# A graph network in fp32: the order of seven products in Strassen's scheme, where their running sums are kept, and 64-column weights for two small products

## The chip, the core and the metric

The kernel runs on one core of a Trainium2 chip. The core has five engines with a queue of instructions each: TensorE (PE) multiplies matrices into PSUM, loading its weights (PEld) beside the multiplications; VectorE (DVE), ScalarE (ACT) and GpSimd (POOL) work element by element; SyncE (SP) issues the transfers (DMA). Engines wait for each other through semaphores, and each engine takes its instructions in the order in which they were written. SBUF is the working memory, PSUM has eight banks of 128 x 512 fp32 words.

The metric is the time of one execution on the device in microseconds, as the median of several runs. A profile is taken of one execution; its span runs from the first instruction to the last.

## What is computed

A chain of four graph layers on x of 128 graphs x 64 nodes x 512 features, with an adjacency matrix adj of 64 x 64 for each graph. Every layer normalizes first, h = max(layernorm(x), 0), and adds its result to x. Cut to what matters:

```python
# layer 0: H = (adj != 0); M = Dn H Be H^T
y = M @ (layernorm(relu(M @ (h @ W1.T) + b1)) @ W2.T) + b2
x = x + y + h
# layer 1: attention weights A (64 x 64) of tanh, leaky relu, exp, adj
x = x + A @ h @ w
# layer 2: attention with adj
q, k, v = h @ Wq.T + bq, h @ Wk.T + bk, h @ Wv.T + bv
p = adj * exp(q @ k.T)
x = x + (p / p.sum(-1)) @ v
# layer 3: transition T (64 x 64); Xk = T^k h
x = x + relu(sum_k(Xk @ Wk[k] + bk[k]))        # k = 0, 1, 2
```

All of it is in fp32.

## The kernel before

Four tiles of 128 tokens (two graphs each) make a group, and there are 16 groups. Layers 0 and 1 go over all groups first and leave x in DRAM (`xmid`); then layers 2 and 3 go over all groups. Large products of two token tiles by a weight matrix are done by Winograd's form of Strassen's scheme: each factor is cut in 2 x 2 blocks, and seven products of blocks stand for eight. A group needs eight such schemes: two each for W1 (512 columns a product), W2 and W (256 columns), then one for q (with the weights Wq and Wk multiplied beforehand, WG) and one for v, both with four multiplications of 256 columns a product. Layer 3 uses the scheme twice over, 7 x 7 products of 128 x 128 blocks for the three weight matrices at once (`product`, L1089), with the factors kept in DRAM (`fac`) and loaded for each use (L1081).

A scheme's left factors are made by four additions on VectorE (`strassen`, `comb`, L642): s1, s2, one in place, and s4. `seven` (L608 to L630) then orders the seven products and the way to the four results. It takes four PSUM banks, p1 to p4. A first product is copied to SBUF by ScalarE (L618) as U0. The sixth goes to p2, and VectorE adds U0 to it as U1 (L620); the seventh goes to p4, and VectorE adds U1 to it as U2 (L622). The second adds to p1 in PSUM, and the result (0,0) is emitted from p1. The fifth goes to p3, and with U2 gives result (1,1). The fourth adds to p4, the third to p3, and these with U1 give (1,0) and (0,1). Three products thus add to a bank that holds an earlier one, and each waits until that one has been read. What an emission does is the caller's: `scaled` with `emit_z` for W1 (L668, L670, relu at L776), `biased` for W2 (GpSimd at L678, VectorE at L680), `emit_w` for W (L842, L843), `emit_q` (L902, L908, L911) and `emit_v` (L951, L953). For q the first copy carries a bias (`first`, L919), and the bias of the other half is mended in two additions with `gb_d`.

The matrix M of layer 0 is made by four multiplications a group (L748, 128 x 128 weights, 65 columns, one for each tile), and T^2 of layer 3 likewise (L1014). Both weights are block diagonal: two graphs of 64 nodes a tile. `left_mul_T` (L586) multiplies h by such a matrix, L801 multiplies y by M, L930 makes the logits of layer 2 with 64-column weights for each half, L1035 multiplies by T and T^2 with 64 rows, L968 multiplies by v. `transposed` turns a tile by a ScalarE copy (L595), a transposing transfer and another copy (L597).

The order of all instructions is settled before the program is written. Each operation is put into a graph with an engine, an assumed cost and a priority; the priority is a running time (`step`) plus a shift for each named part (`AT`) and a period for each group. `Graph.run` goes through a list schedule: it takes the operation that can start earliest by the assumed costs, by priority among equals, and hands out the buffers, PSUM banks too. So a change of one cost or one shift moves instructions on every engine, and the engines then keep to that order whatever they meet. Where the plan leaves TensorE idle for over half a microsecond, `fill` puts multiplications by ones (L1156) there.

Of the kernel before, what the change touches and what calls it, by code (L numbers as in the profile page):

```python
# [14 lines left out]
P = 128  # L15
C = 64
# [152 lines left out]
def tile_adj_preln_d4(  # L169
# [81 lines left out]
    def c_mm(n, count):  # L251
        return 2 * count * max(n * 2 / 2400 + 0.0045, 0.1115)

# [20 lines left out]
    def quad(b):  # L274
# [4 lines left out]

    STRETCH, PERIOD1, PERIOD2 = (3.2256, 5.2241, 17.5226, 2.1512), 108.846, 147.837  # L280
    AT = {
        "x0": -2785.77, "apart": 476.78, "w1": 74.24, "b1": -151.66, "w2": 219.46, "w": 134.54, "c1": 30.0, "l0":
        161.71, "c2": -499.09, "l1": 200.03, "c": 636.68, "g0": -1635.76, "g1": -1647.49, "g2": -1525.11, "g3":
        -1533.9, "g": -74.06, "bq": 140.69, "l3": -1075.2, "wg": -359.01, "wp": 397.89, "beg0": -349.29, "beg1":
        -79.14, "end00": -7.47, "end01": -453.12, "end11": 445.06, "new2": -58.97, "new3": 65.85, "end2": -38.2,
        "end3": 52.04, "load1": -441.32, "load2": -33.39, "m": 8.52, "h0": 1.51, "p0": 16.02, "z0": -2103.65, "q0":
        141.1, "y0": 43.5, "h1": -50.95, "p1": -14.39, "z1": 175.87, "q1": 18.24, "y1": -606.44, "s": 17.3, "t0":
        -515.12, "e0": -376.27, "t1": -24.41, "e1": -275.63, "hT": -120.44, "sh": 574.26, "lq": 31.03, "pt": -20.86,
        "v": -19.97, "pv": -240.05, "s3": 152.28, "tt": 14.82, "a0": 226.63, "b0": -282.82, "a1": 284.86, "ws":
        172.31, "load3": 413.3,  # L290
    }
# [85 lines left out]
    gb_c = const.tile([P, KD], F32, name="gb_c")  # L377
    gb_d = const.tile([P, 2], F32, name="gb_d")
    wg_d = dram.tile([D, D], F32, name="wg_d")

    def dot(in0, in1, acc, r, w):
        j = Buf("o")
        dve(0.77, lambda: nc.vector.scalar_tensor_tensor(j.t, in0(), 1.0, in1(), op0=ALU.mult, op1=ALU.mult,
                                                         accum_out=acc()), r, [*w, j])
# [93 lines left out]
    def setup_bq():  # L478

        pg, bk = Buf("ps"), Buf("o")  # L480
        for o in range(KD):
            k_ = temp(Wk[o * P:(o + 1) * P, :])
            if o == 0:
                dve(0.45, lambda k_=k_: nc.vector.tensor_scalar(bk.t, k_.t, bq_c[:, 0:1], None, op0=ALU.mult), [k_, "bq_c"], [bk])
            else:
                dve(0.77, lambda o=o, k_=k_: nc.vector.scalar_tensor_tensor(bk.t, k_.t, bq_c[:, o:o + 1], bk.t, op0=ALU.mult, op1=ALU.add),
                    [k_, "bq_c", bk], [bk])

        def mg():
            for c in range(KD):  # L490
                nc.tensor.matmul(pg.t[:, c:c + 1], bk.t[:, c * P:(c + 1) * P], ones[:, 0:1], start=True, stop=True)
        pe(c_mm(1, KD), mg, [bk], [pg])
        dve(0.2, lambda: nc.vector.tensor_copy(gb_c, pg.t[:, :KD]), [pg], ["gb"])
        dve(0.16, lambda: nc.vector.tensor_sub(gb_d, gb_c[:, 0:2], gb_c[:, 2:4]), ["gb"], ["gbd"])

# [56 lines left out]
    def norm_stats(src, k, r):  # L552

        st, mv, rs = Buf("st"), Buf("mv"), Buf("rs")
        for i in range(k):
            dve(0.69, lambda i=i: nc.vector.bn_stats(st.t[:, i, :], src(i)), [r[i]], [(st, i)])  # L556
        dve(0.19, lambda: nc.vector.bn_aggr(mv.t, st.t[:, :k, :].rearrange("p k s -> p (k s)")), [(st, i) for i in range(k)], [mv])  # L557
        pool(0.32, lambda: nc.gpsimd.tensor_scalar_add(rs.t, mv.t[:, 1:2], EPS), [mv], [rs])  # L558
        pool(0.65, lambda: nc.gpsimd.tensor_tensor(rs.t, rs.t, mhalf, ALU.pow), [rs], [rs])  # L559
        return mv, rs  # L560

    def offset(mv, rs):
        nm = Buf("nm")
        pool(0.47, lambda: nc.gpsimd.tensor_scalar(nm.t, mv.t[:, 0:1], rs.t, -1.0, op0=ALU.mult, op1=ALU.mult), [mv, rs], [nm])  # L564
        return nm
# [41 lines left out]

    def seven(mul, U, n, emit, first=None):  # L608

        p1, p2, p3, p4 = (Buf("ps") for _ in range(4))
        at = lambda i: (lambda: U.t[:, i, :n])
        mul[1](p1, True)
        if first:
            first(p1)
        else:
            act(n / 1200 + 0.17, lambda: nc.scalar.copy(at(0)(), p1.t[:, :n]), [p1], [(U, 0)])  # L618
        mul[6](p2, True)
        dve(c_v(n), lambda: nc.vector.tensor_add(at(1)(), p2.t[:, :n], at(0)()), [p2, (U, 0)], [(U, 1)])  # L620
        mul[7](p4, True)
        dve(c_v(n), lambda: nc.vector.tensor_add(at(2)(), p4.t[:, :n], at(1)()), [p4, (U, 1)], [(U, 2)])  # L622
        mul[2](p1, False)
        emit(0, 0, p1, None, (U, 0))
        mul[5](p3, True)
        emit(1, 1, p3, (U, 2), (U, 2))
        mul[4](p4, False)
        emit(1, 0, p4, (U, 1), (U, 0))
        mul[3](p3, False)
        emit(0, 1, p3, (U, 1), (U, 1))  # L630

    def strassen(A, keys, B, kc, n, stag, emit, outs=None):
# [8 lines left out]
        def comb(d, kd, x_, kx, y_, ky, op):  # L641
            dve(c_v(kc * P), lambda: nc.vector.tensor_tensor(d(), x_(), y_(), op), [*kx, *ky], kd)  # L642

# [20 lines left out]
    def scaled(dst, wdst, scale, ks, add, ka, p, u, v, n):  # L664

        if u is not None:
            (U, i), j, add0 = u, v[1], add
            dve(c_v(n) + 0.2, lambda: nc.vector.scalar_tensor_tensor(U.t[:, j], U.t[:, i], scale(), add0(), op0=ALU.mult, op1=ALU.add), [u, *ks, *ka], [v])  # L668
            add, ka = (lambda: U.t[:, j]), [v]
        dve(c_v(n, True), lambda: nc.vector.scalar_tensor_tensor(dst(), p.t[:, :n], scale(), add(), op0=ALU.mult, op1=ALU.add), [p, *ks, *ka], [wdst])  # L670

    def biased(dst, j, p, u, v, row, krow):
# [3 lines left out]
        if u is not None:  # L676
            (U, iu), iv = u, v[1]
            pool(0.75, lambda: nc.gpsimd.tensor_add(U.t[:, iv], U.t[:, iu], row()[:, cols]), [u, krow], [v])  # L678
            add, ka = (lambda: U.t[:, iv]), v
        dve(c_v(D // 2, True), lambda: nc.vector.tensor_add(dst.t[:, cols], p.t[:, :D // 2], add()), [p, ka], [(dst, j)])  # L680

# [48 lines left out]
    def layer0(g):  # L730
# [15 lines left out]
        def mm():  # L746
            for t in range(T):
                nc.tensor.matmul(pmv()[:, t, :], HT.t[:, t, :], mB.t[:, t, :], start=True, stop=True)  # L748
        pe(c_mm(65, T), mm, [(HT, 0), (HT, C), mB], [pm])
        for s in HALVES:  # L750
# [55 lines left out]
    def layer1(g):  # L806
# [26 lines left out]
        for t0 in (0, 2):  # L833
# [4 lines left out]
            def emit_w(i, j, p, u, v, t0=t0):  # L838
                xx, cols = xt[g, t0 + i], slice(j * D // 2, (j + 1) * D // 2)
                if u is not None:  # L840
                    U, iu = u
                    pool(0.75, lambda: nc.gpsimd.tensor_add(xx.t[:, cols], xx.t[:, cols], U.t[:, iu]), [xx, u], [xx])  # L842
                dve(c_v(D // 2), lambda: nc.vector.tensor_add(xx.t[:, cols], p.t[:, :D // 2], xx.t[:, cols]), [p, xx], [xx])  # L843

# [8 lines left out]
    def layer2(g):  # L853
# [14 lines left out]
        for q, (a, ka, b, kb, op) in enumerate((  # L868
# [6 lines left out]
              5: (lambda: X.t[:, 2], [(X, 2)]), 6: (lambda: X.t[:, 1], [(X, 1)]), 7: (lambda: X.t[:, 0], [(X, 0)])}  # L875
        pair = lambda f: f.rearrange("p (a n) -> p a n", a=2)

# [20 lines left out]
        def emit_q(i, j, p, u, v):  # L898
# [5 lines left out]
            else:  # L904
                (U, iu), iv = u, v[1]
                at, at0 = (lambda: pair(U.t[:, iv])), (lambda: pair(U.t[:, iu]))
                if i:
                    dve(c_v(D), lambda: nc.vector.tensor_add(at(), pair(p.t), at0()), [p, u], [v])  # L908
                else:
                    for o in range(2):  # L910
                        dve(0.48, lambda o=o: nc.vector.scalar_tensor_tensor(  # L911
                            at()[:, o], pair(p.t)[:, o], gb_d[:, o:o + 1], at0()[:, o], op0=ALU.add, op1=ALU.add), [p, u, "gbd"], [v])
                qs.append((i, j, at, [v]))

        U = Buf("u5")

        def first(p):
            for o in range(2):
                act(0.46, lambda o=o: nc.scalar.activation(pair(U.t[:, 0])[:, o], pair(p.t)[:, o], AF.Identity, bias=gb_c[:, 2 + o:3 + o]), [p, "gb"], [(U, 0)])  # L919

        seven({n: prod(WG[n], hs[n], True) for n in range(1, 8)}, U, D, emit_q, first)

# [22 lines left out]
        def emit_v(i, j, p, u, v):  # L945
# [3 lines left out]
            if u is not None:  # L949
                (U, iu), iv = u, v[1]  # L950
                pool(1.3, lambda: nc.gpsimd.tensor_add(pair(U.t[:, iv]), pair(U.t[:, iu]), bias), [u, "bv_b"], [v])  # L951
                add, ka = (lambda: pair(U.t[:, iv])), v
            dve(c_v(D), lambda: nc.vector.tensor_add(vb[i].t[:, :, at], pair(p.t), add()), [p, ka], [(vb[i], j)])  # L953

# [23 lines left out]
    def layer3(g):  # L978
# [33 lines left out]
        def m2():  # L1012
            for t in range(T):
                nc.tensor.matmul(p2.t[:, t * C:(t + 1) * C], tr.t[:, t, :], tt.t[:, t, 0, :], start=True, stop=True)  # L1014
        pe(c_mm(64, T), m2, [*trk, (tt, 2), (tt, 3)], [p2])
        act(0.38, lambda: nc.scalar.copy(tt.t[:, :, 1, :], p2.t[:, :T * C].rearrange("p (t c) -> p t c", t=T)), [p2], [(tt, 1)])
# [253 lines left out]
```

## Time and profile before

Three runs took 2417.05, 2423.61 and 2429.9 us, a median of 2423.61. The profiled execution took 2414.91 us, of which the span is 2412.9.

| stretch, us | what runs | PE busy | PEld | DVE | ACT | POOL | DMA share |
|---|---|---|---|---|---|---|---|
| 0 to 120 | setup, first groups | 103.62 | 62.12 | 93.24 | 57.02 | 54.69 | 0.55 |
| 120 to 1180 | layers 0 and 1 | 1027.65 | 733.69 | 853.40 | 630.85 | 572.76 | 0.35 |
| 1180 to 1320 | change to layers 2 and 3 | 139.24 | 115.31 | 107.58 | 81.35 | 52.83 | 0.42 |
| 1320 to 2300 | layers 2 and 3 | 963.12 | 892.86 | 844.78 | 525.50 | 468.96 | 0.79 |
| 2300 to 2413 | last groups | 101.94 | 96.78 | 85.92 | 35.55 | 45.84 | 0.63 |

The busy times are in us. A multiplication's length in the trace contains the time in which the next one already runs, so that TensorE's rate is read from the starts of instructions that follow each other. One fp32 multiplication of the program is two instructions in the trace. Names such as `w2m_wm_a_wf` are pieces of memory that several buffers share one after the other: the weights W2 and W first, layer 3's operands and factors later. `u` is U, `s_s_zz` holds the left factors, `y_qT` holds y and later q, `ps` is PSUM.

Groups of the page that the change touches, in instructions and mean length:

| line | engine, what | count | mean ns |
|---|---|---|---|
| L618 | ACT, copy of the first product, 256 / 512 columns | 64 / 48 | 367 / 578 |
| L620 | DVE, running sum U1, 256 / 512 | 64 / 64 | 417 / 683 |
| L622 | DVE, running sum U2, 256 / 512 | 64 / 64 | 415 / 687 |
| L902, L919 | ACT, q with bias, 256 | 32, 32 | 467 (median) |
| L908 | DVE, q's emission, 512 | 32 | 684 |
| L911 | DVE, q's emission with gb_d, 256 | 32 | 479 |
| L748 | PE, M | 128 | 269 |
| L1014 | PE, T^2 | 128 | 269 |

### The profile page before, as it was taken

How to read it: one execution, taken by the hardware profiler on the slowest of the kernel's cores; microseconds unless marked ns; L12 is line 12 of the kernel's file. 1: busy time of each engine (PE TensorE's matmuls, PEld its weight loads, DVE VectorE, ACT ScalarE, POOL GpSimd, SP SyncE). 2: the span in 40 equal slices, each digit the busy share in tenths (PEclk: the TensorE clock that was granted, in tenths of full speed). 3: DMA queues.
4: the chain of work that ended last, by engine and by line, in shares of the span. 5: the costliest groups of instructions: out<-in, count | busy, mean ns of one | idle time of the engine just before them, and what ended most of it. 6: DMA issues, size and time to landing. Idle time of an engine off the chain costs nothing.

```text
span 2412.9 us, 39676 instructions
## 1 busy us (share of the span) xinstructions
PE 2335.6 (97%) x14138; PEld 1900.8 (79%) x14138; DVE 1984.9 (82%) x4084; ACT 1330.3 (55%) x1858; POOL 1195.1 (50%) x1774
## 2 busy tenths in 40 slices
PE   8899999999999999999999999999999999999998
PEld 4676676766677667676688898999999899999988
DVE  7868778788887888778878888888888888888896
ACT  3565655656556565665655565454555555555532
POOL 6225654466655665445533544544544454454444
PEclk9899999999999999999999999999999999999999
DMA  8232333333433343322435877878877777888767
GB/s 273 59 59 71 96 87 83 83 85 103 101 91 87 89 98 78 83 58 53 100 81 149 234 183 218 210 206 236 238 222 208 211 211 210 230 246 213 197 194 230
DMA packets 408374, 359.83 MB, mean 149 GB/s; under 512 B 291185, under 2 KB 326769, under 8 KB 408177
## 3 DMA queue, kind: packets, MB, share of 16 engines
q1 hardware_dynamic: 408176, 357.30, 55.1%
q8 instruction: 111, 1.82, 0.3%
q14 instruction: 87, 0.70, 0.1%
HBM read 245.77 MB, written 44.33 MB: 120 GB/s over the span
## 4 chain that ended last, share of the span: by engine, by line
PE 53%; DVE 16%; DMA 10%; ACT 4%; POOL 4%; issue 2%; SPq 0%; DVEq 0%; POOLq 0%; ACTq 0%
PE ps L650 16%; PE ps L888 13%; PE ps L1089 13%; DMA w2m_wm_a_wf<-fac 5%; PE ps L586 3%; DVE s_s_zz L642 2%; DVE st L556 2%; PE ps L968 2%; DMA adj<-in_adj_dram 2%; PE ps L1035 2%; DVE u L668 2%; DMA h<-o 1%; DVE z_hT L670 1%; PE ps L801 1%; PE ps L930 1%
## 5 line engine op out<-in xcount | busy, mean ns | idle before, releaser
L577 ACT ACTIVATE h<-x,nm,rs 128x512 f32<-128x512 f32 x384 | 303.9, 813 | 183.5 <-POOL nm L564 156.4
L558 POOL TENSOR_SCALAR rs<-mv 128x1 f32<-128x1 f32 x320 | 106.9, 334 | 441.2 <-DVE mv L557 426.9
L1089 PE MATMUL ps<-w2m_wm_a_wf 128*128 128x128 f32 x2304 | 300.1, 276 | 6.2 <-DMA w2m_wm_a_wf<-fac 6.0
L650 PE MATMUL ps<-w2m_wm_a_wf,s_s_zz 128*128 128x256 f32 x1152 | 281.3, 383 | 12.6 <-DVE y_qT L680 11.9
L1089 PEld LDWEIGHTS ps<-w2m_wm_a_wf 128*128 128x128 f32 x2304 | 277.4, 192 | 13.2 <-DMA w2m_wm_a_wf<-fac 5.7
L650 PEld LDWEIGHTS ps<-w2m_wm_a_wf,s_s_zz 128*128 128x128 f32 x1152 | 217.1, 191 | 71.9 <-issue 18.4
L1089 PE MATMUL ps<-w2m_wm_a_wf,tmp_mB_xi 128*128 128x128 f32 x2016 | 263.2, 276 | 6.1 <-DMA w2m_wm_a_wf<-fac 5.5
L1089 PEld LDWEIGHTS ps<-w2m_wm_a_wf,tmp_mB_xi 128*128 128x128 f32 x2016 | 244.8, 192 | 11.3 <-issue 4.5
L650 PE MATMUL ps<-wa_mem,mT_sx 128*128 128x512 f32 x512 | 241.5, 596 | 3.9 <-ACT u L618 3.9
L650 PE MATMUL ps<-w2m_wm_a_wf,rT_wp_vu_tt 128*128 128x256 f32 x1024 | 239.4, 381 | 1.0 <-DVE u L622 1.0
L559 POOL TENSOR_TENSOR rs<-rs,mhalf 128x1 f32<-128x1 f32 x320 | 217.8, 680 | 26.3
L650 PEld LDWEIGHTS ps<-w2m_wm_a_wf,rT_wp_vu_tt 128*128 128x128 f32 x1024 | 193.3, 191 | 36.6 <-issue 9.4
L650 PE MATMUL ps<-wa_mem,s_s_zz 128*128 128x512 f32 x384 | 184.7, 604 | 14.8 <-DVE s_s_zz L642 14.4
L556 DVE BATCH_NORM_STATS2 st<-x 128x6 f32<-128x512 f32 x256 | 173.0, 679 | 11.0 <-DMA x<-xm 5.9
L650 PEld LDWEIGHTS ps<-wa_mem,mT_sx 128*128 128x128 f32 x512 | 95.1, 191 | 100.7 <-issue 91.8
L595 ACT COPY o<-h 128x1024 uint16<-128x1024 uint16 x128 | 133.6, 1045 | 59.7 <-DVE h L1026 52.8
L678 POOL TENSOR_TENSOR u<-u,row_sh 128x256 f32<-128x256 f32 x96 | 74.1, 787 | 175.7 <-DVE u L620 157.9
L597 ACT COPY rT_wp_vu_tt<-z_hT 128x1024 uint16<-128x1024 uint16 x128 | 145.5, 1160 | 24.5 <-DMA z_hT<-tmp_mB_xi 24.1
L586 PEld LDWEIGHTS ps<-bd,h 128*128 128x128 f32 x1024 | 129.7, 194 | 35.0 <-issue 15.9
L564 POOL TENSOR_SCALAR nm<-mv,rs 128x1 f32<-128x1 f32 x320 | 141.1, 441 | 31.3
L788 ACT ACTIVATE z_hT<-z_hT,nm,rs 128x512 f32<-128x512 f32 x128 | 103.8, 812 | 92.1 <-POOL nm L564 91.5
L650 PEld LDWEIGHTS ps<-wa_mem,s_s_zz 128*128 128x128 f32 x384 | 72.1, 192 | 97.1 <-issue 71.1
(189 smaller groups left out, 5152.2 us busy)
## 6 DMA issues: line engine op xcount, KB each, us to landing
w2m_wm_a_wf<-fac SPq DMA_DIRECT2D x112, 768.0 KB, 5.8
w2m_wm_a_wf<-fac SPq DMA_DIRECT2D x112, 576.0 KB, 5.1
x<-xm SPq DMA_DIRECT2D x128, 256.0 KB, 3.4
x<-in_x_dram SPq DMA_DIRECT2D x64, 256.0 KB, 2.8
xm<-x SPq DMA_DIRECT2D x64, 256.0 KB, 2.2
out_dram<-x SPq DMA_DIRECT2D x64, 256.0 KB, 3.1
rT_wp_vu_tt<-in_Wk_dram SPq DMA_DIRECT2D x42, 256.0 KB, 3.1
adj<-in_adj_dram SPq DMA_DIRECT2D x32, 256.0 KB, 3.9
```

The lines of the kernel that those rows point to most:

```text
L556: dve(0.69, lambda i=i: nc.vector.bn_stats(st.t[:, i, :], src(i)), [r[i]], [(st, i)])
L558: pool(0.32, lambda: nc.gpsimd.tensor_scalar_add(rs.t, mv.t[:, 1:2], EPS), [mv], [rs])
L559: pool(0.65, lambda: nc.gpsimd.tensor_tensor(rs.t, rs.t, mhalf, ALU.pow), [rs], [rs])
L564: pool(0.47, lambda: nc.gpsimd.tensor_scalar(nm.t, mv.t[:, 0:1], rs.t, -1.0, op0=ALU.mult, op1=ALU.mult), [mv, rs], [nm])
L577: act(0.82, lambda: nc.scalar.activation(h.t, xx.t, AF.Relu, bias=nm.t, scale=rs.t), [xx, nm, rs], [h])
L586: nc.tensor.matmul(quad(p)[:, c, :], h.t[:, c * P:(c + 1) * P], rhs(), start=True, stop=True)
L595: act(1.05, lambda: nc.scalar.copy(u16(planes.t).rearrange("p (q c) -> p q c", q=2), u16(src()).rearrange("p (c q) -> p q c", q=2)), ksrc, ...
L597: act(1.16, lambda: nc.scalar.copy(u16(dst()).rearrange("p c (k q) -> p c k q", q=2), u16(back()).rearrange("p (q c r) -> p c r q", q=2, c ...
L650: nc.tensor.matmul(p.t[:, :n], lhs()[:, c, :], rhs(c), start=first and c == 0, stop=c == kc - 1, skip_group_check=True)
L788: act(0.72, lambda half=half, rs=rs, nm=nm: nc.scalar.activation(half(), half(), AF.Identity, bias=nm.t, scale=rs.t), [(z, j), rs, nm], [( ...
L888: nc.tensor.matmul(pair(p.t)[:, o, :], a, b, start=first and o == 0 and c == 0, stop=c == 1, skip_group_check=True)
L1089: nc.tensor.matmul(inner(p, q)[:, r, :], at()[:, k, :], w_.t[:, r, k, :], start=first and r == 0 and k == 0, stop=k == 2, skip_group_check ...
```

## The change

`seven` takes three banks. The running sums are no longer made by VectorE: the products 1, 6, 7 and 4 all add to one bank, px, and after each of the first three ScalarE copies the bank's content to SBUF (`snap`), as U0, U1 and U2. The second product has a bank py of its own; the fifth goes to pz and is copied, and the third adds to pz. The result (0,0) is now product 2 plus U0, (1,1) is the copied fifth plus U2, (0,1) is pz plus U1, and (1,0) is px as it stands. For q the copies carry the bias (of one half for U0 and U1, of the other for U2), and `gb_d` goes; the copy of the fifth goes to a `qT` buffer there. M and T^2 are multiplied in two halves of 64 weight columns for each tile. Assumed costs in the planner change (TensorE's a little lower; GpSimd's, `comb`'s and `dot`'s higher), and so do the priorities of all parts.

```diff
@@ costs
-        return 2 * count * max(n * 2 / 2400 + 0.0045, 0.1115)
+        return 2 * count * max(n * 2 / 2412 + 0.0015, 0.1105)
...
-    STRETCH, PERIOD1, PERIOD2 = (3.2256, 5.2241, 17.5226, 2.1512), 108.846, 147.837
+    STRETCH, PERIOD1, PERIOD2 = (2.2716, 3.2191, 45.0793, 4.0782), 120.976, 138.654
...
-            dve(c_v(kc * P), lambda: nc.vector.tensor_tensor(d(), x_(), y_(), op), [*kx, *ky], kd)
+            dve(c_v(kc * P) * 1.12, lambda: nc.vector.tensor_tensor(d(), x_(), y_(), op), [*kx, *ky], kd)
...
-            pool(0.75, lambda: nc.gpsimd.tensor_add(U.t[:, iv], U.t[:, iu], row()[:, cols]), [u, krow], [v])
+            pool(0.89, lambda: nc.gpsimd.tensor_add(U.t[:, iv], U.t[:, iu], row()[:, cols]), [u, krow], [v])
@@ seven
-        p1, p2, p3, p4 = (Buf("ps") for _ in range(4))
-        at = lambda i: (lambda: U.t[:, i, :n])
-        mul[1](p1, True)
-        if first:
-            first(p1)
-        else:
-            act(n / 1200 + 0.17, lambda: nc.scalar.copy(at(0)(), p1.t[:, :n]), [p1], [(U, 0)])
-        mul[6](p2, True)
-        dve(c_v(n), lambda: nc.vector.tensor_add(at(1)(), p2.t[:, :n], at(0)()), [p2, (U, 0)], [(U, 1)])
-        mul[7](p4, True)
-        dve(c_v(n), lambda: nc.vector.tensor_add(at(2)(), p4.t[:, :n], at(1)()), [p4, (U, 1)], [(U, 2)])
-        mul[2](p1, False)
-        emit(0, 0, p1, None, (U, 0))
-        mul[5](p3, True)
-        emit(1, 1, p3, (U, 2), (U, 2))
-        mul[4](p4, False)
-        emit(1, 0, p4, (U, 1), (U, 0))
-        mul[3](p3, False)
-        emit(0, 1, p3, (U, 1), (U, 1))
+        px, py, pz = (Buf("ps") for _ in range(3))
+        fifth = fifth or (U, 0)
+        def snap(p, v, i=None):
+            if biased_by and i is not None:
+                for o in range(2):
+                    act(0.46, lambda o=o: nc.scalar.activation(pair(pv(v))[:, o], pair(p.t)[:, o], AF.Identity, bias=biased_by(i, o)), [p, "gb"], [v])
+            else:
+                act(n / 1200 + 0.17, lambda: nc.scalar.copy(pv(v)[:, :n], p.t[:, :n]), [p], [v])
+        mul[1](px, True)
+        snap(px, (U, 0), 0)
+        mul[2](py, True)
+        emit(0, 0, py, (U, 0), (U, 0))
+        mul[6](px, False)
+        snap(px, (U, 1), 0)
+        mul[5](pz, True)
+        snap(pz, fifth)
+        mul[7](px, False)
+        snap(px, (U, 2), 1)
+        emit(1, 1, fifth, (U, 2), (U, 2))
+        mul[3](pz, False)
+        emit(0, 1, pz, (U, 1), (U, 1))
+        mul[4](px, False)
+        emit(1, 0, px, None, (U, 0))
@@ M (T^2 likewise)
-                nc.tensor.matmul(pmv()[:, t, :], HT.t[:, t, :], mB.t[:, t, :], start=True, stop=True)
-        pe(c_mm(65, T), mm, [(HT, 0), (HT, C), mB], [pm])
+                for s in HALVES:
+                    nc.tensor.matmul(pmv()[s, t, :], HT.t[:, t, s], mB.t[:, t, :], start=t == 0, stop=True, skip_group_check=True)
+        pe(0.7, mm, [(HT, 0), (HT, C), mB], [pm])
@@ emit_q
-                (U, iu), iv = u, v[1]
-                at, at0 = (lambda: pair(U.t[:, iv])), (lambda: pair(U.t[:, iu]))
-                if i:
-                    dve(c_v(D), lambda: nc.vector.tensor_add(at(), pair(p.t), at0()), [p, u], [v])
-                else:
-                    for o in range(2):
-                        dve(0.48, lambda o=o: nc.vector.scalar_tensor_tensor(
-                            at()[:, o], pair(p.t)[:, o], gb_d[:, o:o + 1], at0()[:, o], op0=ALU.add, op1=ALU.add), [p, u, "gbd"], [v])
+                at = lambda: pair(pv(v))
+                dve(c_v(D), lambda: nc.vector.tensor_add(at(), pair(pv(p)), pair(pv(u))), [p, u], [v])
```

In the changed file the same operations stand at other lines: L626 is the copy of a product (L618 before) and L624 the one with a bias, L654 is `comb` (L642), L662 the product of a scheme (L650), L692 is y's emission (L680), L749 is the first reading of adj for M (L737), L761 is M (L748), L1016 is T^2 (L1014), L1158 the filler (L1156).

## The prediction

> **What bounds the kernel now.** I read the page's first part, then the order of time on TensorE, then what TensorE waits for.
>
> ```profile
> span 2412.9 us, 39676 instructions
> ...
> PE 2335.6 (97%) x14138; PEld 1900.8 (79%) x14138; DVE 1984.9 (82%) x4084; ACT 1330.3 (55%) x1858; POOL 1195.1 (50%) x1774
> ...
> PEclk9899999999999999999999999999999999999999
> ```
>
> TensorE is the bound, but 97% is a modelled busy time and hides stalls. The pitch of its instructions is the better measure (order of time, TensorE alone: start, length, engine, line, operation, count, idle before):
>
> ```profile
> 711.99 1.88 PE L650 MATMUL ps<-wa_mem,mT_sx 128*128 128x512 f32 x4
> 713.71 1.05 PE L586 MATMUL ps<-bd,h 128*128 128x128 f32 x8
> 714.60 1.89 PE L650 MATMUL ps<-w2m_wm_a_wf,rT_wp_vu_tt 128*128 128x256 f32 x8
> 716.33 1.05 PE L586 MATMUL ps<-bd,h 128*128 128x128 f32 x8
> 718.08 1.98 PE L650 MATMUL ps<-wa_mem,s_s_zz 128*128 128x512 f32 x4 [0.69 <-DVE s_s_zz L642]
> ```
>
> From start to start: 1.72/4 = 0.429 us for 512 columns, 1.73/8 = 0.216 for 256, 0.89/8 = 0.112 for 128. Counts of the page's groups times pitch: 4704 (L1089) x 0.112 = 527; 4480 (L650, L888) x 0.216 = 968; 1056 (L650, L801, L469) x 0.429 = 453; 1024 + 256 (L586, M, T^2) x 0.112 = 143; L968, L930, L1035 and small ones 153. That is 2244 us of needed work; the 278 fillers of L1156 add 31. So 2413 - 2244 - 31 = 138 us are stalls. The same sum by stretches of the span gives 28 in 0-120, 49 in 120-1180 (layers 0 and 1), 3 in 1180-1320, 43 in 1320-2300 (layers 2 and 3), 15 at the end. Everything the change can win is in those 138 and in the needed work.
>
> Where the 49 come from (order of time, all engines):
>
> ```profile
> 841.27 0.81 ACT L788 ACTIVATE z_hT<-z_hT,nm,rs 128x512 f32<-128x512 f32 x1 [4.98 <-POOL nm L564]
> 841.62 0.59 DVE L737 TENSOR_SCALAR bd<-adj 64x256 f32<-64x256 f32 x2 [2.21 <-DMA adj<-in_adj_dram]
> ...
> 842.44 0.42 DVE L680 TENSOR_TENSOR y_qT<-ps,u 128x256 f32<-128x256 f32 x1
> ...
> 842.91 2.04 PEld L650 LDWEIGHTS ps<-w2m_wm_a_wf,s_s_zz 128*128 128x128 f32 x8 [2.47 <-DVE y_qT L680]
> 842.91 2.76 PE L650 MATMUL ps<-w2m_wm_a_wf,s_s_zz 128*128 128x256 f32 x8 [2.07 <-DVE y_qT L680]
> ```
>
> The third product of W2 goes into bank p3 and must wait until the emission of the fifth (L680, VectorE) has read it; L680 stands behind L737, which waits for adj. Start to start this class costs 14 us. The next ones (waits of TensorE):
>
> ```profile
> PE ps L650 <- DVE s_s_zz L642: 15.1, 14, 3.9
> PE ps L1089 <- DMA w2m_wm_a_wf<-fac: 12.3, 25, 1.4
> PE ps L650 <- DVE y_qT L680: 11.9, 13, 2.3
> PE ps L452 <- ACT row_sh L445: 4.9, 1, 4.9
> ```
>
> VectorE is behind two of the three that recur.
>
> **What the Trainium skill says.** "Perfetto Trace Analysis", Identifying the Most-Contended Engine: matmul busy time is a bad measure because matmuls are pipelined; the 276 ns shown for a 128-column L1089 against its 112 ns pitch agrees. "PSUM — Partial Sum Buffer", PSUM bank collisions: a bank is guarded by semaphores as a whole, so a product that adds to a bank waits for the copy out of it. The 2.07 us above is such a wait. "TensorEngine Tiling (Array Packing)", Key Properties: different tiles run in parallel, and changing the mode drains TensorE; both show at L930 below. "GPSIMD Engine Reference", its table of specifications: SBUF interfaces are shared with VectorE, contended when a VectorE instruction has two SBUF inputs; L642 has two, and ranges from 0.40 to 1.48 us at equal size.
>
> **The change part by part**, against the profiled span of 2412.9.
>
> *Running sums in PSUM.* VectorE loses L620 and L622: 64 x 0.683 + 64 x 0.687 + 64 x 0.417 + 64 x 0.415 = 141 us; with q's emissions (32 x 0.684 + 32 x 0.479 become 48 x 0.684) 145, so 1985 goes to 1840, 76%. The fifth product's emission now reads two SBUF operands; if these 128 lose 0.16 each to GpSimd (L642's mean over its median), 20 us come back. ScalarE gains 192 copies x 0.367, 160 x 0.578, 64 biased x 0.467 = 193: 1330 goes to 1523, 63%. GpSimd's adds stay at the same count. None of this is on the path by itself; what counts is who holds TensorE. The L680 class goes, because the fifth product is copied out at once by ScalarE and the y emissions free a bank that nobody adds to next: -13 (bounds -14 and 0). The s4 waits (L642, 12.5 us in steady state) stay a VectorE matter. VectorE is relieved by 6 us per group in layers 0 and 1, so I take -5 (bounds -12 and 0).
>
> In their place stand four ScalarE gates per scheme, 1-6, 6-7, 7-4 and 5-3, 512 in all, where before there were one on ScalarE and two on VectorE. A gate needs 0.20 us from the product's end to the copy, 0.37 or 0.58 for the copy, 0.05 back: 0.62 or 0.83. In the built order the work between the two products on a bank is 1.73 us or more nearly everywhere and 0.87 once per group, as before. A copy that is late stands behind a longer instruction: L577 0.81, L595 1.05, L597 1.16. The 112 old copies cost TensorE 4.7 us, 0.042 each; 512 at this rate are 21.5. I take 12, since much of it falls on slots with spare time, less the 10 of L618, L622 and L908 that go: +2 (bounds -8 and +25).
>
> *64-column weights for M and T^2.* 16 + 16 places of 4 multiplications become 8. Nearest row is L930, of that very form (order of time, TensorE):
>
> ```profile
> 1529.36 1.89 PE L888 MATMUL ps<-wa_mem,row_sh 128*128 128x256 f32 x8
> 1531.18 0.69 PE L930 MATMUL ps<-y_qT,z_hT 128*64 128x64 f32 x16
> 1531.70 1.57 PE L930 MATMUL ps<-u,z_hT 128*64 128x64 f32 x48
> 1533.20 1.99 PE L888 MATMUL ps<-wa_mem,row_sh 128*128 128x256 f32 x8
> ...
> 1541.94 1.00 PE L1014 MATMUL ps<-rT_wp_vu_tt,bd 128*128 128x64 f32 x8
> 1542.78 1.09 PE L968 MATMUL ps<-rT_wp_vu_tt,bd 128*128 128x257 f32 x4
> ```
>
> L930: 2.02/64 = 0.0316 each, plus 0.09 to enter (1531.18 - 1529.36 - 8 x 0.216). New: 16 x 0.0316 + 0.09 = 0.60 against 0.84: -0.24 x 32 = -8 (bounds -13 without any drain, 0 with twice the drain).
>
> *q's bias on ScalarE* is in the sums above; losing gb_d is nothing. *The product emitted from PSUM without a running sum* is now (1,0) instead of (0,0): same count.
>
> *Order anew.* SyncE issues the same 1153 instructions, and an adj load still stands between the two halves of a row's way through DRAM, so no transfer is added. The built order shows L749 (old L737) behind the y emissions, not in front; its first reader of adj is now the row sum L835. In layers 2 and 3 a group has 1 filler instead of 3: -0.45 x 13 = -6. The total of fillers goes from 139 to 180 multiplications (two instructions each), the increase lying in the first 200 us, at the change to layers 2 and 3, and before the last T^2; where they stand the planner leaves TensorE idle, so +41 x 0.22 = 9, of which 6 is already counted off: +15 for those three places, and I take half, +8, because start and end already had 28 and 15 us of stalls. The planner's GpSimd costs rise to what the trace has (L678 0.787 plus 0.08 to the next against 0.75 old, 0.89 new), so its order should hold better: -9 out of the 49 + 43 steady stalls (bounds -25 and +15; an order moves everything and can lose as well).
>
> Sum: -13 - 5 + 2 - 8 - 6 + 8 - 9 = -31, so 2382 in a profile. The profiled run was 2414.9 and the median of the runs 2423.6; on that median 2393.
>
> **Rivals.** *A half of it hidden* (same): the relief of VectorE only brings the next waits forward, fac transfers (12.3) and h, z; what stays is M, T^2 and half of L680: -15 + 8 = -7, 2417. For it: in layers 2 and 3 VectorE holds TensorE hardly at all. Against: L680 has no other cause behind it. *ScalarE becomes the gate* (slower): ScalarE takes instructions in order, and its queue has long waits, 4.98 us for nm above, 110 us in total of L776 on VectorE. In the new order 101 of the copies stand directly behind an L577 and 54 behind an L776. If one copy in four of the 512 is 0.5 us late beyond its slack, that is 64 us, less the 33 won elsewhere: 2455. The gains are used up at 33/512 = 0.064 us per gate, and it is slower by over 0.5% from (33 + 12)/512 = 0.088 on, twice the old 0.042. Behind a late copy also stand the copies of h M (L588) and both halves of each transpose (L595, L597), for which the products of W2 wait. Against: 37% of ScalarE is still free, and the gate is one hop where the old one went through GpSimd and VectorE. *The stalls mostly go* (faster): steady stalls fall from 92 to 45, 2413 - 8 - 47 - 6, on the median 2362.
>
> **Numbers.** Forecast 0.57 (own range 2372 to 2411), mostly gone 0.10, hidden 0.14, ScalarE 0.19. 0.5%, 12 us, is about what can be told from no change. Faster 0.67, same 0.14, slower 0.19. The range from 2355 to 2437 leaves out most of the ScalarE case and the outer end of the best one.
>
> **What would show it.** VectorE near 1840 and ScalarE near 1523 busy; no wait of TensorE on L692 (old L680) above 3 us; M and T^2 at some 0.6 us a place; steady stalls of 60 to 80 us. It is wrong if TensorE's waits on the copies (L626) exceed 40 us, or if start, change of layers and end lose over 20 us.

## The result and the profile after

The changed kernel took 2411.51 us (median of 8 runs, 2407.44 to 2416.39) against 2428.24 for the kernel before in the same session: a ratio of 0.9937, with a 95% interval from 0.9918 to 0.9955. The forecast was 31 us; 17 came (15 by the ratio). The direction was right, the size about half.

The two profiled executions lie closer together, 2414.91 and 2408.39 us: the one of the kernel before was 13 us below the median of its runs, the other 3 us below its own. What follows from the profiles thus accounts for 6.6 us of span, not for 17.

The page of the changed kernel, its span and the busy time of each engine:

```profile
span 2406.3 us, 40384 instructions
...
PE 2331.3 (97%) x14476; PEld 1893.0 (79%) x14476; DVE 1896.4 (79%) x3811; ACT 1496.8 (62%) x2274; POOL 1230.2 (51%) x1774
```

ScalarE rose by 166 us and VectorE fell by 88; 193 and, with 20 coming back, 125 had been reckoned. What TensorE waits for (total, times, longest):

```profile
PE ps L662 <- ACT u L626: 13.2, 9, 2.8
PE ps L662 <- DVE s_s_zz L654: 10.2, 15, 1.4
...
PE ps L900 <- ACT z_hT L595: 6.2, 9, 1.6
```

The wait on y's emission (L680 before, L692 now), 11.9 us, has left the list. In its place stands one on ScalarE's copies, 13.2 us in only nine waits; that on the s additions (L642 before, L654 now) went from 15.1 to 10.2.

Time by the work done. For each profile I noted when so many us of needed TensorE work (instructions times pitch, M, T^2 and fillers left out) had been started:

| needed work, us | before, at us | after, at us | difference |
|---|---|---|---|
| 100 | 133.7 | 144.3 | +10.6 |
| 1200 (into layer 2) | 1309.4 | 1309.2 | -0.2 |
| 2180 (last group) | 2362.9 | 2349.9 | -13.0 |
| 2215 (the end) | 2403.8 | 2397.1 | -6.6 |

So, in this pair of profiles, the start lost 10.6 us, layers 0 and 1 won 10.8, layers 2 and 3 won 12.8, and the last group lost 6.4. By the stretches of the prediction, the stalls of layers 0 and 1 (120 to 1180 us) went only from 49 to 42.

Where a good part of those 42 comes from is seen in the order of time of one group, all engines (start, length, what was waited for). In the changed file L680 and L682 are the two steps of W1's emission; y's emission, L680 before, is L692:

```profile
421.92 1.44 POOL L778 TENSOR_TENSOR x<-x,h 128x512 f32<-128x512 f32 x1
422.16 1.48 DVE L654 TENSOR_TENSOR s_s_zz<-mT_sx,s_s_zz 128x256 f32<-128x256 f32 x1
423.44 1.33 POOL L779 TENSOR_TENSOR x<-x,row_sh 128x512 f32<-128x512 f32 x1
423.56 1.75 DVE L680 SCALAR_TENSOR_TENSOR u<-u,col,row_sh 128x512 f32<-128x512 f32 x1
...
425.35 0.75 DVE L682 SCALAR_TENSOR_TENSOR z_hT<-ps,col,u 128x512 f32<-128x512 f32 x1
...
426.14 0.63 ACT L789 ACTIVATE z_hT<-z_hT 128x512 f32<-128x512 f32 x1 [5.15 <-DVE z_hT L682]
...
426.68 1.06 ACT L626 COPY u<-ps 128x512 f32<-128x512 f32 x2
...
427.30 1.98 PE L662 MATMUL ps<-wa_mem,s_s_zz 128*128 128x512 f32 x4 [2.17 <-ACT u L626]
```

Read from the bottom. TensorE waits for a copy. The copy stands behind a relu (L789) that had waited 5.15 us for VectorE's L682. VectorE was late because an s addition took 1.48 us, where the median is 0.42, and L680 took 1.75. Both began just after an addition of GpSimd in layer 0 (L778: x + h; L779: + b2) and ended 0.28 and 0.54 us after it. The wait list names ScalarE; the time was lost between VectorE and GpSimd. Six of the nine waits on L626, 10.8 of the 13.2 us, have this chain: a relu that waited for L682, and ahead of it instructions of VectorE that overlap L778 or L779 and take 0.8 to 1.8 us. The Trainium skill, "SBUF — State Buffer", section "SBUF: two separate sides", says that these two share a pair of ports that one instruction holds for its whole length, when VectorE's has two operands in SBUF. The lines agree: each of the two VectorE instructions ends only after GpSimd's addition has ended. That took about 1 us from each.

### The profile page after: what moved, and what is told of

It is laid out like the page before. It is cut to its first block, busy times and chain, and to the rows that moved or that the text cites. A ratio compares the mean times of both kernels' runs of the same rounds, so it can differ in the third digit from the quotient of the medians.

```text
span 2406.3 us, 40384 instructions
## 1 busy us (share of the span) xinstructions
PE 2331.3 (97%) x14476; PEld 1893.0 (79%) x14476; DVE 1896.4 (79%) x3811; ACT 1496.8 (62%) x2274; POOL 1230.2 (51%) x1774
## 4 chain that ended last, share of the span: by engine, by line
PE 62%; DVE 15%; DMA 11%; ACT 7%; issue 2%; POOL 2%; SPq 0%; DVEq 0%; POOLq 0%; ACTq 0%
PE ps L662 26%; PE ps L900 12%; PE ps L1091 12%; DMA h<-o 4%; PE ps L584 3%; PE ps L1037 2%; DVE o L382 2%; DVE s_s_zz L654 2%; ACT h L575 2%; PE ps L814 2%; DVE st L554 2%; PE ps L969 1%; ACT o L593 1%; DMA rw<-row 1%; PE ps L931 1%
## 5 line engine op out<-in xcount | busy, mean ns | idle before, releaser
L626 ACT COPY u<-ps 128x256 f32<-128x256 f32 (+1 forms) x448 | 203.4, 462 | 212.4 <-PE ps L662 133.5
L556 POOL TENSOR_SCALAR rs<-mv 128x1 f32<-128x1 f32 x320 | 114.0, 356 | 359.7 <-DVE mv L555 312.7
L662 PE MATMUL ps<-w2m_wm_a_wf,s_s_zz 128*128 128x256 f32 x1152 | 275.0, 380 | 3.7 <-DVE x L856 1.5
L662 PEld LDWEIGHTS ps<-w2m_wm_a_wf,s_s_zz 128*128 128x128 f32 x1152 | 216.7, 190 | 54.9 <-issue 20.0
L662 PE MATMUL ps<-wa_mem,mT_sx 128*128 128x512 f32 x512 | 244.5, 601 | 3.8 <-DMA wa_mem<-in_W1T_dram 3.0
L662 PE MATMUL ps<-w2m_wm_a_wf,rT_wp_vu_tt 128*128 128x256 f32 x1024 | 242.3, 381 | 3.8 <-ACT rT_wp_vu_tt L595 3.8
L662 PEld LDWEIGHTS ps<-w2m_wm_a_wf,rT_wp_vu_tt 128*128 128x128 f32 x1024 | 194.4, 191 | 63.3 <-issue 32.3
L662 PE MATMUL ps<-wa_mem,s_s_zz 128*128 128x512 f32 x384 | 180.5, 600 | 20.5 <-ACT u L626 11.5
L690 POOL TENSOR_TENSOR u<-u,row_sh 128x256 f32<-128x256 f32 x96 | 79.5, 829 | 223.4 <-ACT u L626 223.4
L554 DVE BATCH_NORM_STATS2 st<-x 128x6 f32<-128x512 f32 x256 | 175.2, 689 | 21.4 <-DMA x<-xm 11.2
L662 PEld LDWEIGHTS ps<-wa_mem,mT_sx 128*128 128x128 f32 x512 | 96.1, 192 | 91.2 <-issue 81.4
L593 ACT COPY o<-h 128x1024 uint16<-128x1024 uint16 x128 | 134.1, 1047 | 43.4 <-DVE h L1028 22.0
L1100 ACT COPY s_s_zz<-ps 128x512 f32<-128x512 f32 (+1 forms) x128 | 68.1, 533 | 136.6 <-PE ps L1091 136.5
L855 POOL TENSOR_TENSOR x<-x,u 128x256 f32<-128x256 f32 x96 | 75.2, 784 | 149.1 <-ACT u L626 148.6
```

The costliest lines, as they stand in the source:

```text
L556: pool(0.40, lambda: nc.gpsimd.tensor_scalar_add(rs.t, mv.t[:, 1:2], EPS), [mv], [rs])
L593: act(1.05, lambda: nc.scalar.copy(u16(planes.t).rearrange("p (q c) -> p q c", q=2), u16(src()).rearrange("p (c q) -> p q c", q=2)), ksrc, ...
L626: act(n / 1200 + 0.17, lambda: nc.scalar.copy(pv(v)[:, :n], p.t[:, :n]), [p], [v])
L662: nc.tensor.matmul(p.t[:, :n], lhs()[:, c, :], rhs(c), start=first and c == 0, stop=c == kc - 1, skip_group_check=True)
L690: pool(0.89, lambda: nc.gpsimd.tensor_add(U.t[:, iv], U.t[:, iu], row()[:, cols]), [u, krow], [v])
```

## The experiments

Times are compared by their ratio to the kernel before; 0.001 is 2.4 us.

**128 columns for M and T^2 again**, everything else as changed, the order the same (M is shown; T^2 likewise):

```diff
-                for s in HALVES:
-                    nc.tensor.matmul(pmv()[s, t, :], HT.t[:, t, s], mB.t[:, t, :], start=t == 0, stop=True, skip_group_check=True)
+                nc.tensor.matmul(pmv()[:, t, :], HT.t[:, t, :], mB.t[:, t, :], start=True, stop=True)
```

> The changed kernel with M and T^2 multiplied in 128 weight columns again, in the same order on every engine. Theory (the 64-column form is a real gain on TensorE's path): a place goes from 16 x 0.030 + 0.2 of entering and leaving = 0.68 us to 8 x 0.112 = 0.90, 32 places: +7 us, ratio to the kernel before 0.9966 against 0.9937. Rival 1 (the time is hidden in waits that stand beside these places): 0 to +2 us, ratio 0.9937 to 0.9945. Rival 2 (entering and leaving the 64-column form costs more than those 0.2 us): -3 us or better, ratio below 0.993.

Measured 0.9891 (0.9876 to 0.9905), 2395.45 us: faster by 0.0046, 11 us, where every theory but the last had it slower or level. The place itself did what had been reckoned. TensorE alone, changed kernel:

```profile
412.53 1.03 PE L662 MATMUL ps<-w2m_wm_a_wf,mT_sx 128*128 128x256 f32 x4
413.49 0.69 PE L761 MATMUL ps<-tmp_mB_xi,bd 128*64 128x65 f32 x16
414.11 1.98 PE L662 MATMUL ps<-wa_mem,mT_sx 128*128 128x512 f32 x4
```

From 412.53 plus 4 x 0.216 to 414.11 are 0.71 us: 0.09 to enter, 0.47, and 0.15 from the last start to the next, of which 0.12 is leaving. In 128 columns the same place takes 0.84. So rival 2 is wrong about the place, and still the kernel is faster without the shorter form. The stalls fell instead, the waits on L626 from 13.2 us, those on L654 from 10.2:

```profile
PE ps L662 <- ACT u L626: 9.5, 8, 1.7
...
PE ps L662 <- DVE s_s_zz L654: 6.6, 14, 1.2
```

The same group in this kernel (its lines from L760 on stand one lower):

```profile
414.53 0.94 DVE L654 TENSOR_TENSOR s_s_zz<-mT_sx,s_s_zz 128x256 f32<-128x256 f32 x1
...
415.15 1.44 POOL L777 TENSOR_TENSOR x<-x,h 128x512 f32<-128x512 f32 x1
415.39 1.75 DVE L680 SCALAR_TENSOR_TENSOR u<-u,col,row_sh 128x512 f32<-128x512 f32 x1
...
417.96 0.63 ACT L788 ACTIVATE z_hT<-z_hT 128x512 f32<-128x512 f32 x1 [3.70 <-DVE z_hT L682]
...
419.12 0.70 PE L662 MATMUL ps<-wa_mem,s_s_zz 128*128 128x512 f32 x1 [1.19 <-ACT u L626]
```

Here the s addition starts 0.62 us ahead of GpSimd's addition, not 0.24 behind it. Of the two, only L680 meets one of the layer's additions, and TensorE waits 1.19 us instead of 2.17.

**A 64-column place as long as the 128-column one** (the first tile is multiplied twice; T^2 likewise):

```diff
-            for t in range(T):
+            for t in (0, *range(T)):
```

> The changed kernel with its 64-column form of M and T^2, and one tile multiplied twice in each place, so that a place lasts 0.71 + 4 x 0.030 = 0.83 us, as long as in 128 columns (0.84); the order on every engine stays. Theory 1 (what counts is when the work behind the place starts: VectorE and GpSimd meet on other instructions, and the 128-column run was better for that alone): 8 to 14 us faster than the changed kernel, nearly all won in layers 0 and 1, ratio 0.988 to 0.990. Theory 2 (the 64-column form itself harms what follows): 4 us slower than the changed kernel, ratio 0.995 to 0.996.

Measured 0.9921 (0.9903 to 0.9940): outside the figures of both theories, and by the time not to be told from the changed kernel. In the profile, from the mark of 100 us of needed work to the end, it won 11.2 us on the changed kernel, 128 columns 10.6. That speaks for theory 1, though only 7.6 of the 11.2 were won in layers 0 and 1. Ahead of that mark 128 columns also won 5 us, and this one lost 2. A part of that is the granted clock: in the first 120 us half rate (see the last section) took 8.5 us of the clock in the changed kernel, 6.8 with 128 columns and 11.9 here. The rest stays open. A place that is made to last longer did not make the kernel slower.

**GpSimd's two additions taken away** but for one column of 512, the order the same (x + h is shown; + b2 likewise):

```diff
-nc.gpsimd.tensor_add(xx.t, xx.t, h.t)
+nc.gpsimd.tensor_add(xx.t[:, :1], xx.t[:, :1], h.t[:, :1])
```

> The changed kernel with GpSimd's two additions of a tile in layer 0 (x + h, + b2, L778 and L779, 64 each) done on one column instead of 512: that part of the result is left out, the order stays. Theory (the stalls on ScalarE's copies L626 in layers 0 and 1 come from VectorE: its s additions and L680 are stretched while GpSimd adds, the relu on ScalarE waits for them, and the copy stands behind the relu): VectorE's L654 on 256 columns falls from a mean of 0.54 us to below 0.47, TensorE's waits on L626 and L654, 25 us together, to below 12, the end comes 12 to 20 us earlier, ratio 0.986 to 0.989. Rival (the gates wait for ScalarE's own queue): the waits on L626 stay at 12 us or more, 0 to 4 us earlier, ratio 0.992 to 0.994.

Measured 0.9796 (0.9775 to 0.9817), 2372.05 us: 0.0141, 34 us, better than the changed kernel, more than the theory said. Its waits:

```profile
PE ps L900 <- ACT z_hT L595: 11.8, 11, 1.8
...
PE ps L662 <- ACT u L626: 2.0, 3, 0.7
...
PE ps L662 <- DVE s_s_zz L654: 1.7, 2, 1.3
```

Both lines together fell from 23.4 to 3.7 us, the stalls of layers 0 and 1 from 42 to 15.5, and VectorE's busy time to 1835.8. The s additions fell less in the mean (0.44 to 0.51 us at 256 columns, 0.51 to 0.58 before) than expected. So ScalarE's queue was not what held the copies.

**GpSimd held, but away from SBUF** (five additions of one column for each of the two; + b2 likewise):

```diff
-nc.gpsimd.tensor_add(xx.t, xx.t, h.t)
+[nc.gpsimd.tensor_add(xx.t[:, :1], xx.t[:, :1], h.t[:, :1]) for _ in range(5)]
```

> As e_lean, with five additions of one column in place of each of GpSimd's two additions of 512 (the same part of the result is left out): GpSimd is held as long as by the whole additions (5 x 0.30 to 0.34 us against 1.43), but hardly touches SBUF. Theory (VectorE's instructions are stretched because both engines want SBUF): nearly as fast as e_lean, 2370 to 2385 us, ratio 0.979 to 0.984. Rival (what e_lean won was GpSimd's time: rs and nm, for which ScalarE waits, came earlier): most of the gain is gone, 2400 us or more, ratio 0.991 or more.

Measured 0.9812 (0.9791 to 0.9834), 2375.87 us. Groups by line (count | busy, mean ns):

```profile
L778 POOL TENSOR_TENSOR x<-x,h 128x1 f32<-128x1 f32 x320 | 87.2, 273 | 28.2 <-ACT h L575 8.1
L779 POOL TENSOR_TENSOR x<-x,row_sh 128x1 f32<-128x1 f32 x320 | 80.3, 252 | 25.9 <-DMA row_sh<-in_b_dram 2.0
```

GpSimd is busy with these for 168 us, against 183 with the whole additions, and the gain stays. So the additions cost TensorE next to nothing by the time that they hold GpSimd; what costs is the width of what they read and write in SBUF.

**The same in the kernel before:**

> The kernel before with the same two additions of GpSimd (x + h, + b2) done on one column; that part of the result is left out, the order stays. Theory 1 (the kernel before paid less for them than the changed one, 39 us, so that the new order met more of these encounters and gave back part of the gain): 10 to 25 us faster than before, ratio 0.990 to 0.996. Theory 2 (it paid as much; the two meet in every order): 33 to 45 us faster, ratio 0.981 to 0.986. The difference to e_lean is what the change is worth without them.

Measured 0.9823 (0.9799 to 0.9848): 43 us faster than before, theory 2. Stalls of layers 0 and 1 fell from 49 to 11. The wait on L680 fell from 11.9 to 4.7 us, though its bank and its emission are as they were:

```profile
PE ps L650 <- DVE y_qT L680: 4.7, 5, 1.2
```

So most of the wait that the change was credited with removing goes with the additions too. The way is not a direct one: in the kernel before nine of the 13 waits on L680 stand behind VectorE's wait for adj, as the prediction read, and all five that are left here do. How the additions make more of these waits reach TensorE is not shown. Without the additions, changed against before is 0.9796 to 0.9823, some 6.5 us. The other 8.7 of the changed kernel's 15 us would be encounters that it has fewer of. By the intervals of the four ratios both figures are uncertain by 8 to 9 us, so that the change by itself is not shown to be worth anything.

**Three kernels, with and without the additions.** The setup priorities of the kernel before were put into the changed kernel, then together with 128 columns, and the additions were taken from the kernel with 128 columns and from the one with both:

```diff
-        "x0": -3806.98, "apart": 498.48, "w1": -320.93, "b1": -1275.93, "w2": -171.37, "w": 45.2, "c1": -3695.71,
+        "x0": -2785.77, "apart": 498.48, "w1": 74.24, "b1": -151.66, "w2": 219.46, "w": 134.54, "c1": 30.0,
...
```

> The changed kernel with the priorities of the setup parts and of the first group as in the kernel before. Theory (the new order of the setup, with Wk and Wq loaded late, is what loses the start): 100 us of needed work are done at 134 us of the span instead of 144, and the end comes 8 to 10 us earlier, ratio 0.990. Rival 1 (the new scheme itself is slow while the pipeline is empty): still 142 to 146 us at that mark, ratio 0.993 to 0.995. Rival 2 (what the start loses, later waits take back): 134 us at that mark, but the end only 0 to 3 us earlier.

> 128 columns for M and T^2 and the setup priorities of the kernel before, together. Theory 1 (two causes, which add: 5 us of start by the priorities and 10 us of layers 0 and 1 by the 128 columns): 2390 us or less, ratio 0.985 to 0.988. Theory 2 (both only moved the moment at which VectorE and GpSimd meet; together they may meet anywhere): ratio 0.989 to 0.994.

> 128 columns for M and T^2 with the two additions of GpSimd done on one column (left out of the result as in e_lean). If the 11 us by which 128 columns won were a matter of whom GpSimd's additions meet, they are gone: 0 to 5 us slower than e_lean, since a place is 0.13 us longer, ratio 0.979 to 0.982. If the 128-column form helps by itself: 8 us or more faster than e_lean, ratio below 0.9765.

> 128 columns and the setup priorities of the kernel before, with the two additions of GpSimd done on one column (left out of the result as in e_lean). With the whole additions this one was 22 us slower than 128 columns alone. If that spread comes from whom the additions meet: within 8 us of the 128-column kernel with the same part left out, on either side. If the order of the setup is bad with 128 columns for another reason: still 15 us or more slower than it.

| kernel | ratio | without the additions |
|---|---|---|
| changed | 0.9937 | 0.9796 |
| 128 columns | 0.9891 | 0.9809 |
| old setup priorities | 0.9916 | not run |
| both | 0.9972 | 0.9832 |

The setup priorities alone do at the start what was said: 100 us of work at 134.1 us instead of 144.3. In the time they are worth 5 us (0.9916 against 0.990 expected, interval 0.9901 to 0.9931, which overlaps with that of the changed kernel). With 128 columns as well, the kernel is slower than either and than the changed one, outside both theories: between the marks of 100 and 300 us of work it loses 15 us on the changed kernel. Without the additions, 128 columns are no longer faster than the changed form (0.9809 against 0.9796): the 11 us are gone, as was expected if they came from whom the additions meet. The three stand within 0.0036, 9 us, where they had stood within 0.0081, 20 us. The remaining 6 us between the last two are just inside what had been expected (8).

**The kernel before with 64 columns**, the same order:

> The kernel before with M and T^2 in 64 weight columns and nothing else; the order on every engine stays as it was. Theory 1 (the place is 0.13 us shorter and the rest follows): 32 x 0.13 = 4 us faster, ratio 0.998; by the reckoning of the prediction 8 us, 0.997. Theory 2 (a shift of 0.13 us a group changes which instructions of VectorE and GpSimd meet, by more than it saves): outside 0.9965 to 1.0000, on either side, with the difference in stalls of layers 0 and 1. Theory 3 (the 64-column form harms what follows): slower by 5 us or more, ratio above 1.002.

Measured 1.0002 (0.9988 to 1.0017): no gain, and not slower by 5 us, so theory 3 is out. The figures of theory 1, 0.998 and 0.997, lie outside the interval as well; the bound of theory 2, 1.0000, lies within it, so that theory 2 is not shown. In the profile the end stands 12 us later, with 62 us of stalls in layers 0 and 1 instead of 49; but this execution was 4 us above the median of its runs and that of the kernel before far below its own, so the pair proves little.

**Fillers, and the last group's priorities:**

```diff
-        for _ in range(int(gap * FILL / (0.224 if filled else 0.448))):
+        for _ in range(0):
```

> The changed kernel without its 180 fillers, 40 us of TensorE; nothing of the result depends on them. Theory (they stand where TensorE would wait anyway): -5 to +5 us, ratio 0.992 to 0.996; the waits grow by what the fillers took. Rival 1 (they push needed work back, as at the q products that wait behind one): -9 to -20 us, ratio 0.985 to 0.990. Rival 2 (without them the granted clock falls after idle stretches): slower, over +15 us, with a clock below 0.98 in some stretch.

> The changed kernel with the shifts of the last group in layers 2 and 3 (end2, end3) as in the kernel before. Theory (the new order of the last group is what loses the end): the last 35 us of needed work take 4 to 6 us less, ratio 0.9915. Rival (the end is held by the chain of the last layer 3, whatever the order): 0 +- 2 us, ratio 0.993 to 0.9945.

Without fillers 0.9937 (0.9923 to 0.9950): nothing in the time. The clock did fall, as rival 2 had it: from 120 to 2380 us half of it was granted for 30.7 us, against 3.4 in the changed kernel, and from 2340 to 2380 the mean was 0.87. It cost nothing that can be seen. With the old priorities of the last group 0.9945 (0.9930 to 0.9961): nothing either, so what costs the last group 6 us stays open. This second kernel has the changed kernel's order up to the last group, and its marks up to there lie within 3 us of it. That is one pair; the runs of the kernel before spread over 18 us (2416.93 to 2435.07), so a difference of a few us between two profiles proves nothing.

**Every copy of a product made twice** (those with a bias likewise):

```diff
-                act(n / 1200 + 0.17, lambda: nc.scalar.copy(pv(v)[:, :n], p.t[:, :n]), [p], [v])
+                act(n / 1200 + 0.17, lambda: [nc.scalar.copy(pv(v)[:, :n], p.t[:, :n]) for _ in range(2)], [p], [v])
```

> The changed kernel with every copy of a product made twice by ScalarE, in the same order, and with GpSimd's two additions in layer 0 done on one column (left out of the result as in e_lean), so that the gates are seen without those encounters. ScalarE gains 186 us, 1494 to 1680. Theory (a gate has slack; TensorE waits on copies only where VectorE held ScalarE up): the waits on L626, 2.5 us in e_lean, rise to 6 to 12, the end comes 5 to 15 us later than e_lean, ratio 0.982 to 0.986. Rival (ScalarE is nearly the gate of the new scheme): one gate in four gets 0.37 us or more later, 48 us or more, ratio 0.999 or more.

> The changed kernel, nothing left out, with every copy of a product made twice by ScalarE, in the same order. Theory (slack in the gates, but the delays fall on the queue that already waits for VectorE): 10 to 25 us slower than the changed kernel, ratio 0.998 to 1.004. Rival (ScalarE is nearly the gate): 48 us or more, ratio 1.0135 or more.

Measured 0.9962 (0.9949 to 0.9974) without the additions, 40 us above 0.9796; and 1.0090 (1.0069 to 1.0112) with them, 37 above the changed kernel. Both theories missed, on either side: ScalarE rose by 242 us (1493.7 to 1735.9), and 40 of them, 0.16 of each, reached TensorE. The gates have slack, but it is used up for a good part of them; there is no room for a second copy.

## Why the prediction was right about the sign and wrong about the size

The step that failed is how the prediction got VectorE off TensorE's path: it took -13 for L680, priced the copies that stand in its place at +2 as a matter of ScalarE's own queue, and held in the first rival that "L680 has no other cause behind it". Its second rival saw the path, the relu's waits for VectorE (L776, 110 us), but the sum did not use it. It left out GpSimd's additions, though it had their price in hand: L642 "ranges from 0.40 to 1.48 us at equal size". What TensorE waits for from 120 to 1180 us, two lines of the kernel before and two of the changed one:

```profile
PE ps L650 <- DVE s_s_zz L642: 11.2, 13, 1.9
PE ps L650 <- ACT u L618: 3.9, 5, 1.1
...
PE ps L662 <- ACT u L626: 12.5, 8, 2.8
PE ps L662 <- DVE s_s_zz L654: 9.1, 14, 1.4
```

L680's 11.9 us went, the s additions gave 2.1, and the copies took 8.6 back. Without the additions (the run with one column in place of 512) the copies have 0.7 us here and the s additions 0.4.

- *L680, -13.* The wait went, as said, and L692 shows none above 0.7 us. But VectorE's lateness stayed and now reaches TensorE through the relu and the copies. Stalls of layers 0 and 1 fell by 7 us in the profiles, where -13 - 5 and the share of -9 that falls there made some -23.
- *s additions, -5.* By the wait list -4.9 over the whole span. VectorE's relief was priced too high: 145 less 20, and its busy time fell by 88; without the additions too it fell by only 86 (1921.6 to 1835.8). The forecast took a sum of lengths from a busy time, but neighbouring instructions overlap in the trace: the sum of lengths did fall by 118, and L620 and L622, 141 us in length, cover 121 us of busy time in the trace of before.
- *Gates, +2.* L618, L622 and L908, 10 us as the prediction has it, went; L626 came with 13.2. Of these only 2.0 are there without the additions. ScalarE as the gate (2455 us) did not happen; it took a second copy everywhere to come near (2447.66).
- *M and T^2, -8.* The place won 0.13 us, not 0.24: the leaving, 0.12, was left out though the row of L930 showed it. That is 4 us, and on the path even the sign was not given: 11 us the wrong way in the changed kernel (none of it without the additions), no gain in the kernel before.
- *Fillers, -6.* Without any of them the time is the same.
- *Start, change and end, +8.* It was 10.6 + 6.4 = 17. The old setup order gives the start back (134.1 us at the mark). Without the additions the changed order stands there at 134.6 and the kernel before at 128.1: by one profile each, some 6 us of the loss stay without the additions.
- *Order holds better, -9.* The planner's new costs are means. They cannot say that the same addition takes 0.42 us or 1.48 by what GpSimd does; a better mean bought nothing that could be seen.

Layers 2 and 3 won 12.8 us, near what the steps for them gave (fillers, T^2 and parts of the gates and the order: some 13), but only in part for the reasons given: the run without fillers shows no gain from them, and 1.7 us are a stretch at half clock (see the last section) that only the kernel before had there.

That the sign came out right was in part luck. The prediction did not reckon the encounters of VectorE and GpSimd, and by the middle values over half of the gain lies there. The same scheme with 128 columns and the old setup priorities gave 0.9972, 7 us.

Of the kernels that compute everything, the changed scheme with 128 columns is the fastest: 0.9891, below both.

## What to carry to other kernels

When a wait list names an engine, follow that engine's own wait back until an instruction is longer than its median; here three hops led from a copy to GpSimd. Look at the spread of equal instructions (0.42 and 1.48 us) before pricing a change: where two engines hold each other up, the time of a kernel with a fixed order moved by 11 us when 32 places changed by 0.13 us each, and by 20 between orders of its setup, so an edit that saves 4 us can't be told by its sum. A single pair of profiles can't tell it either, where the runs of one kernel spread over 18 us. Take such an encounter away in both kernels first, then compare.

## What the runs showed of the hardware

TensorE often goes to half its rate after a wait of over 2 us. TensorE alone, changed kernel:

```profile
728.81 2.66 PE L662 MATMUL ps<-wa_mem,s_s_zz 128*128 128x512 f32 x4 [2.83 <-ACT u L626]
731.26 2.95 PE L662 MATMUL ps<-wa_mem,mT_sx 128*128 128x512 f32 x4
734.05 1.89 PE L662 MATMUL ps<-w2m_wm_a_wf,s_s_zz 128*128 128x256 f32 x8
```

From 728.81 to 734.05 eight instructions take 5.24 us, where 8 x 0.429 = 3.43 is right: three of them start 0.85 us apart, twice the pitch, and the wait of 2.83 us costs 1.8 more. The trace also records the granted clock, as a share of full speed. In one stretch (from and to, its length, each engine's busy time with its instructions, then the clock and the DMA share):

```profile
730.10:733.30 3.20, 3.20 (x5) 1.35 (x4) 2.13 (x6) 1.38 (x3) 1.89 (x5) 0.50 0.01 3
```

Half the clock was granted from 730.0 on, for 3.41 us. In the sixteen profiles every such stretch ahead of the last 12 us is 3.41 us long, or two, three or four times that. Between the first 100 and the last 12 us one began during the wait, or within 2 us of its end, for 14 of 17 waits of 2.3 us or more, for 8 of 17 from 2.0 to 2.3, and for 7 of 198 from 1.0 to 2.0. The Trainium skill, "TensorE: Matmul & The Clock Gate", Part 1, describes a half rate after an idle window of about 3.4 us that runs freely; that a wait of the same length (2.83 us before 577.65, the same kernel) costs nothing fits a free-running window, that 2.3 us are often enough does not fit its length. So a wait just above 2 us is dearer than it looks.

This is a part of the spread between the kernels: from 120 to 1180 us half rate took 6.8 us of the clock in the kernel with both edits (0.9972), 5.1 in the kernel before, 1.7 in the changed one, and none with 128 columns or in any kernel without the additions.
